# A scan's carry kept in PSUM by writing the capped product one column to the left

## The chip, the cores and the metric

The kernel runs on one core of a Trainium2 chip. The metric is the device time of one launch in microseconds (us); several launches are timed and the median is given. A core has five engines with their own queues: TensorE (PE in the profile) for matrix products, VectorE (DVE), ScalarE (ACT) and GpSimd (POOL) for elementwise work, and SyncE (SP), which here only issues transfers. SBUF is the working memory on the chip, PSUM the small memory into which TensorE writes.

## The reference, cut to what matters

The input has 32 images of 96 channels, 56 x 56 positions. The first layer is a ConvNeXt block: a 7 x 7 convolution per channel, a normalisation over the channels, two dense layers with a GELU between them, and a residual. The second layer, which the change touches, is a 5 x 5 convolution per channel with SiLU, and then a selective scan over the L = 3136 positions of each image, with N = 4 states per channel:

```python
delta = softplus(einsum('dr,brl->bdl', dt_w, dts) + dt_b)
A = -exp(A_logs)
log_dA = maximum(delta[:, :, None, :] * A[None, :, :, None], LOG_EPS)
P = exp(cumsum(log_dA, axis=-1))
dB_u = delta[:, :, None, :] * Bs[:, None, :, :] * xs[:, :, None, :]
hs = P * cumsum(dB_u / maximum(P, EPS), axis=-1)
y = einsum('bdnl,bnl->bdl', hs, Cs) + xs * Ds
```

P is a running product of decays along the positions, and EPS is 1e-9. The kernel carries P/EPS instead of P: where it has fallen below 1, the reference's floor EPS is in force. It computes hs by a recurrence, hs[t] = decay[t] * hs[t-1] + min(P[t]/EPS, 1) * dB_u[t]. The factor with the minimum is called the capped product here.

## The kernel before, in words

The work is done in four stages, one after the other, with intermediate results in HBM: the first convolution, the dense layers (mlp), the second convolution, and the scan. The change is in the scan stage alone.

The scan stage takes each image in two halves of CH = 1568 positions. A step is one half of one image. A pair of images goes together: both first halves, then both second halves. The 96 channels are taken in NG = 3 groups of 32, and 32 channels with 4 states each fill the 128 partitions. One group of one step is a unit: 64 steps x 3 groups make 192 units. Their order has a period of twelve units: six units of first halves (q = 0; two images, three groups), then six of second halves (q = 1).

A unit needs a tile `rep` with two planes: the decay and the drive. It is loaded by SP from HBM (`spread_du`), where delta and delta times x were put before (`keep_du`). ACT turns delta into the decay in three passes (`decay`, L648 to L650). POOL multiplies the drive by B (`drive`, L654). Then DVE does the scan (`scan`): a first scan (L661) forms the running product in the PSUM tile `pv`, with a column of zeros as the other operand; a product with a minimum (L666) caps it, multiplies it by the drive and writes it in place; a second scan (L670) forms hs. In first halves a copy (L665) saves the last column of the running product in `carry_p`, an SBUF tile of six columns, one for each of the six units; the unit of the second half starts its first scan from it. The carry of hs is saved by POOL in `carry_h` (L680).

After that POOL weighs hs with C (`weigh`, L681), PE sums over the states and adds the skip term (`gather`, L687 and L694), and ACT copies the result out of PSUM and issues its store (`store`, L704 and L705). PE also prepares B and C for each step (`rows_bc`, `spread`) and the input of the softplus (`delta_in`); ACT does the softplus (`delta`, L593), POOL the product of delta and x (`delta_x`, L599).

The order is written out by hand. One loop over units, with lead-in and tail, calls these functions at fixed distances: the load four units ahead of the scan, the decay two ahead, the drive one ahead, the weighing one behind. `pin` keeps the order of the calls on each engine. Tiles in pools are reused in turn: five buffers for `rep`, five for hs. The tile `pv` has one buffer of 2048 columns[...]; the running product takes its first 1568 columns and the zero is its last.

Of the kernel before, what the change touches and what calls it, by code (L numbers as in the profile page):

```python
# [8 lines left out]
F32 = mybir.dt.float32  # L9
AF = mybir.ActivationFunctionType  # L10
ALU = mybir.AluOpType
# [21 lines left out]
CH = 1568  # L33
NI = 2
NCH = L // CH
# [3 lines left out]
EPS = 1e-9  # L39
# [3 lines left out]
NG = 3  # L43
# [3 lines left out]
def convnext_then_scan_kernel(  # L47
# [22 lines left out]
    nc = tc.nc  # L70
    pin = tc.keep_in_program_order
# [70 lines left out]
    with tc.tile_pool(name="prep", bufs=1) as prep, tc.tile_pool(  # L142
        name="prep_ps", bufs=1, space=PSUM
# [7 lines left out]
        at = H - 1 - K1 // 2  # L151
# [62 lines left out]
        for k in range(4):  # L214
            rows = slice(32 * k, 32 * k + 2 * N)
            at = 32 * k + (k // 2) * N
# [34 lines left out]
    with tc.tile_pool(name="c1", bufs=3) as pool, tc.tile_pool(  # L251
        name="c1k", bufs=1
# [15 lines left out]
        for c in range(C):  # L268
# [41 lines left out]
            acc2, in0=sq, scalar=-1.0 / C, in1=acc2, op0=ALU.mult, op1=ALU.add  # L310
# [11 lines left out]
    with tc.tile_pool(name="mlp", bufs=2) as pool, tc.tile_pool(  # L322
        name="mlp_h", bufs=3, space=PSUM
# [115 lines left out]
    with tc.tile_pool(name="c2", bufs=3) as pool, tc.tile_pool(  # L439
        name="c2k", bufs=1  # L440
# [93 lines left out]
    with tc.tile_pool(name="sc", bufs=2) as pool, tc.tile_pool(  # L534
        name="sc_k", bufs=1, space=PSUM
    ) as ps_k, tc.tile_pool(name="sc_ps", bufs=2, space=PSUM) as psum:

        pv = ps_k.tile([128, 2048], F32, name="pv")
        nc.vector.memset(pv, 0.0)
        zero = pv[:, 2047:2048].to_broadcast([128, CH])  # L540
        run = pv[:, :CH]
        steps = B * NCH
        units = steps * NG
        xts: dict = {}
# [5 lines left out]
        hss: dict = {}  # L550
        pzs: dict = {}
        pys: dict = {}
        carry_p = pool.tile([128, NI * NG], F32, name="carry_p", bufs=1)
        carry_h = pool.tile([128, NI * NG], F32, name="carry_h", bufs=1)
        HQ = H // NCH

        def place(k):

            p, i = divmod(k, NI)
            return p // NCH * NI + i, p % NCH  # L560
# [95 lines left out]
        def scan(i):  # L656
            k, g = divmod(i, NG)
            q, col = place(k)[1], k % NI * NG + g
            da, ut = (reps[i][:, j, :] for j in range(2))

            pin(nc.vector.tensor_tensor_scan(  # L661
                run, da, zero, carry_p[:, col : col + 1] if q else 1.0 / EPS, ALU.mult, ALU.add
            ))
            if q < NCH - 1:
                pin(nc.vector.tensor_copy(carry_p[:, col : col + 1], run[:, CH - 1 : CH]))  # L665
            pin(nc.vector.scalar_tensor_tensor(  # L666
                run, in0=run, scalar=1.0, in1=ut, op0=ALU.min, op1=ALU.mult
            ))
            ht = pool.tile([128, CH], F32, name=f"hs_{i}", tag="hs", bufs=5)
            pin(nc.vector.tensor_tensor_scan(  # L670
                ht, da, run, carry_h[:, col : col + 1] if q else 0.0, ALU.mult, ALU.add
            ))
            hss[i] = ht
# [41 lines left out]
        for i in range(-12, units + 2):  # L715

            p, at = divmod(i + 8, PER)
# [31 lines left out]
            if 0 <= p < PC and 1 <= at <= 4:  # L749
                j, h = halves[at - 1]  # L750
                delta_x(p * NI + j, h)
            at_unit(i, scan)
            if g == 0 and 0 <= after < steps:
                gather(after, 0)
# [46 lines left out]
```

## Time and profile before

| What | us |
|---|---|
| median of 3 runs | 3668.39 |
| lowest and highest | 3664.61, 3669.38 |
| the profiled execution, its time | 3661.97 |
| the profiled execution, its span | 3660.2 |
| first scan (L661) starts, last scan (L670) ends, in the span | 1888.5, 3646.0 |
| DVE busy in the span | 2670.0 |
| L661, first half / second half, 96 each | 3.428 / 3.489 each |
| L665, 96 | 0.157 each |
| L666, 192 | 1.800 each |
| L670, first half / second half, 96 each | 3.420 / 3.480 each |

The profile is one execution taken by the hardware's profiler. A row names the line of the kernel, the engine, the operation, the tile written, an arrow, and the tiles read; then come shapes and counts, the busy time, and how long the engine stood idle just before and what ended that. An idle time in brackets in a view by time means the same. The span is divided in 40 equal slices in one view, where each digit is the busy share of a slice in tenths.

### The profile page before, as it was taken

How to read it: one execution, taken by the hardware profiler on the slowest of the kernel's cores; microseconds unless marked ns; L12 is line 12 of the kernel's file. 1: busy time of each engine (PE TensorE's matmuls, PEld its weight loads, DVE VectorE, ACT ScalarE, POOL GpSimd, SP SyncE). 2: the span in 40 equal slices, each digit the busy share in tenths (PEclk: the TensorE clock that was granted, in tenths of full speed). 3: DMA queues.
4: the chain of work that ended last, by engine and by line, in shares of the span. 5: the costliest groups of instructions: out<-in, count | busy, mean ns of one | idle time of the engine just before them, and what ended most of it. 6: DMA issues, size and time to landing. Idle time of an engine off the chain costs nothing. (4 is left out here: it accounts for less than half of the span.)

```text
span 3660.2 us, 46554 instructions
## 1 busy us (share of the span) xinstructions
PE 3054.0 (83%) x17290; PEld 1284.6 (35%) x17290; DVE 2670.0 (73%) x1867; ACT 2343.2 (64%) x2133; POOL 1951.4 (53%) x1241
## 2 busy tenths in 40 slices
PE   7999996899999999899948777777777777777775
PEld 5777774333333333334312222222222222222221
DVE  5666665233333333699949999999999999999998
ACT  3555553333333333588858888888888888888884
POOL 2333331122222222100038998898898898898896
PEclk9999998899999999999966666667667667667666
DMA  5555553455555554699977877877877877877873
GB/s 153 167 167 169 168 166 108 150 162 162 160 163 160 162 158 121 183 285 292 289 235 251 276 245 272 275 258 262 272 250 266 277 256 262 278 253 265 278 256 109
DMA packets 302055, 790.70 MB, mean 216 GB/s; under 512 B 123012, under 2 KB 180164, under 8 KB 277156
## 3 DMA queue, kind: packets, MB, share of 16 engines
q1 hardware_dynamic: 259076, 669.31, 56.6%
q0 software_dynamic: 28416, 79.87, 7.2%
q10 hardware_dynamic: 14336, 38.54, 2.8%
q8 instruction: 137, 2.24, 0.3%
q14 instruction: 90, 0.74, 0.1%
HBM read 551.83 MB, written 235.74 MB: 215 GB/s over the span
## 5 line engine op out<-in xcount | busy, mean ns | idle before, releaser
L681 POOL TENSOR_TENSOR hs<-hs,ct 128x1568 f32<-128x1568 f32 x192 | 672.9, 3505 | 102.8 <-DVE hs L670 91.0
L654 POOL TENSOR_TENSOR rep<-rep,bt 128x1568 f32<-128x1568 f32 x192 | 674.5, 3513 | 14.5 <-DMA rep<-du_d 14.5
L382 ACT ACTIVATE g<-ph,b1p_t 128x896 f32<-128x896 f32 x336 | 320.1, 1004 | 512.2 <-PE ph L372 512.2
L402 DVE SCALAR_TENSOR_TENSOR o<-po,b2r_t,x 128x224 f32<-128x224 f32 x336 | 190.5, 609 | 572.3 <-PE po L391 572.3
L286 PE MATMUL ps<-xq,wt 120*112 120x448 f32 x1536 | 581.2, 539 | 14.4 <-POOL xq L281 14.4
L414 POOL DMA_DIRECT2D block_d<-o x336 | 183.0, 552 | 703.8 <-DVE o L402 621.8
L286 PEld LDWEIGHTS ps<-xq,wt 120*112 120x112 f32 x1536 | 429.4, 280 | 165.9 <-POOL xq L281 14.6
L372 PE MATMUL ph<-h,w1r_t 32*128 32x448 f32 x4032 | 440.1, 559 | 55.7 <-DVE h L362 54.0
L599 POOL TENSOR_TENSOR du<-du,xs 96x784 f32<-96x784 f32 x128 | 236.2, 1846 | 367.1 <-ACT du L593 367.1
L585 PE MATMUL pz<-xs,wd_t 96*96 96x392 f32 x512 | 268.6, 688 | 182.6 <-ACT du L593 147.9
L391 PE MATMUL po<-g,w_t 128*32 128x448 f32 x4032 | 413.1, 543 | 0.0
L694 PE MATMUL py<-hs,sel_t 128*32 128x392 f32 x1536 | 330.0, 680 | 85.5 <-POOL hs L681 85.5
L661 DVE TENSOR_TENSOR_SCAN pv<-rep,pv 128x1568 f32<-128x1568 f32 x96 | 329.1, 3428 | 59.9 <-DMA rep<-du_d 43.3
L666 DVE SCALAR_TENSOR_TENSOR pv<-pv,rep 128x1568 f32<-128x1568 f32 x192 | 345.6, 1800 | 21.1 <-POOL hs L681 1.4
L630 PE MATMUL pk<-bn,pick_t 8*128 8x392 f32 x1024 | 284.9, 672 | 87.2 <-ACT y L704 68.1
L661 DVE TENSOR_TENSOR_SCAN pv<-rep,carry_p,pv 128x1568 f32<-128x1568 f32 x96 | 334.9, 3489 | 9.5 <-DVE hs L670 0.5
L670 DVE TENSOR_TENSOR_SCAN hs<-rep,carry_h,pv 128x1568 f32<-128x1568 f32 x96 | 334.1, 3480 | 10.0
L480 PE MATMUL ps<-xq,wt 128*32 128x448 f32 x3072 | 308.4, 547 | 34.2 <-DMA xq<-block_d 31.8
L670 DVE TENSOR_TENSOR_SCAN hs<-rep,pv 128x1568 f32<-128x1568 f32 x96 | 328.4, 3420 | 9.9 <-PE pk L630 0.5
L503 DVE COPY st<-yt 28x896 f32<-28x896 f32 x288 | 317.6, 1103 | 20.6 <-ACT yt L494 8.5
L687 PE MATMUL py<-xs,dsm_t 96*96 96x392 f32 x512 | 318.9, 768 | 14.5 <-ACT bn L618 9.5
L648 ACT ACTIVATE rep<-rep,a_t 128x1568 f32<-128x1568 f32 x192 | 308.4, 1606 | 12.5 <-DMA rep<-du_d 12.2
(87 smaller groups left out, 3473.1 us busy)
## 6 DMA issues: line engine op xcount, KB each, us to landing
rep<-du_d SPq DMA_DIRECT2D x192, 1568.0 KB
du_d<-du SPq DMA_DIRECT2D x128, 588.0 KB
xq<-block_d SPq DMA_DIRECT2D x192, 225.0 KB
block_d<-o POOLq DMA_DIRECT2D x336, 120.0 KB, 5.6
xt<-in_x_dram SPq DMA_DIRECT2D x192, 196.0 KB
h<-conv_d SPq DMA_DIRECT2D x84, 448.0 KB
x<-in_x_dram SPq DMA_DIRECT2D x336, 112.0 KB
conv_d<-st SPq DMA_DIRECT2D x96, 392.0 KB
```

What stands on the lines that cost most here:

```text
L286: nc.tensor.matmul(ps[:, j, :PQ].rearrange("p (i r) -> p i r", i=BI), lhsT=wv[:KR, t], rhs=xq[:KR, j, :, t : t + W2], start=(t == 0), stop ...
L372: pin(nc.tensor.matmul(phs[i // 2][:, i % 2, :HALF], lhsT=w1r_t[rows, d, f * 128 : (f + 1) * 128], rhs=hts[n, d][rows, s * HALF : (s + 1) ...
L382: nc.scalar.activation(gt, ph[:, :, :HALF], AF.Gelu, bias=b1p_t[:, f : f + 1], scale=1.0)
L391: pin(nc.tensor.matmul(po[CB * i : CB * i + CB, :HALF], lhsT=w2_t[:, f, CB * d : CB * d + CB], rhs=gts[n, s, f, i // 2][:, i % 2], start=( ...
L503: pin(copy(st[:, :, :, :, f], yt[RW * f : RW * f + QR].rearrange("p h (b q) -> p h b q", q=QW),))
L654: pin(nc.gpsimd.tensor_mul(ut, ut, bts[i // NG]))
L661: pin(nc.vector.tensor_tensor_scan(run, da, zero, carry_p[:, col : col + 1] if q else 1.0 / EPS, ALU.mult, ALU.add))
L666: pin(nc.vector.scalar_tensor_tensor(run, in0=run, scalar=1.0, in1=ut, op0=ALU.min, op1=ALU.mult))
L670: pin(nc.vector.tensor_tensor_scan(ht, da, run, carry_h[:, col : col + 1] if q else 0.0, ALU.mult, ALU.add))
L681: pin(nc.gpsimd.tensor_mul(ht, ht, cts[k]))
L687: pin(nc.tensor.matmul(half(py[:C], s), lhsT=dsm_t, rhs=tokens(k, 2 * h + s, 4), start=True, stop=False,))
L694: pin(nc.tensor.matmul(py[g * DG : (g + 1) * DG, s, :BK], lhsT=sel_t, rhs=hss[k * NG + g][:, cols], start=False, stop=True, tile_position= ...
```

## The change

The running product is written one column to the right of where the capped product is put. Let `at` be the column at which the capped product begins. The first scan writes columns `at + 1` to `at + 1568`, and the product with the minimum reads these and writes `at` to `at + 1567`. So the last column of the running product, `at + 1568`, is left as it was. In first halves `at` is 6, 5, 4, 3, 2 and 1 for the six units in their order, so each unit's last column lies just behind the columns that the later units use, and the six carries stand in columns 1569 to 1574. In second halves `at` is 0, and the highest column written is 1568. The first scan of a second half takes its start value from the unit's column in PSUM. The tile `carry_p` and the copy into it are gone. The zero stays in column 2047. After the change the first scan has line 664, the product line 667, the second scan line 671.

```diff
-        run = pv[:, :CH]
...
-        carry_p = pool.tile([128, NI * NG], F32, name="carry_p", bufs=1)
...
             da, ut = (reps[i][:, j, :] for j in range(2))
+            at = 0 if q else NI * NG - col
+            run, grown = pv[:, at : at + CH], pv[:, at + 1 : at + 1 + CH]
+            last = NI * NG - col + CH
 
             pin(nc.vector.tensor_tensor_scan(
-                run, da, zero, carry_p[:, col : col + 1] if q else 1.0 / EPS, ALU.mult, ALU.add
+                grown, da, zero, pv[:, last : last + 1] if q else 1.0 / EPS, ALU.mult, ALU.add
             ))
-            if q < NCH - 1:
-                pin(nc.vector.tensor_copy(carry_p[:, col : col + 1], run[:, CH - 1 : CH]))
             pin(nc.vector.scalar_tensor_tensor(
-                run, in0=run, scalar=1.0, in1=ut, op0=ALU.min, op1=ALU.mult
+                run, in0=grown, scalar=1.0, in1=ut, op0=ALU.min, op1=ALU.mult
             ))
```

## The prediction

> **What bounds the kernel now.** I read the strip of 40 slices first, to find the stage that the change touches, and then asked for the busy time of each engine between the first scan's start and the last scan's end.
>
> ```profile
> DVE  5666665233333333699949999999999999999998
> ```
> ```profile
> 1888.50:3646.00 1757.50, 1308.11 (x4536) 409.94 (x4536) 1687.07 (x672) 1427.04 (x1202) 1574.53 (x602) 0.67 0.77 259
> ```
>
> The columns of the second fence are the window, its length, then busy time and count of PE, weight loads, VectorE (DVE), ScalarE (ACT) and GpSimd (POOL), the clock, the DMA share and GB/s. In the scan stage DVE is busy 1687.1 of 1757.5 us (96%), POOL 90%, ACT 81%, PE 74%, DMA 77%. The rest of DVE's time is mostly the step from one instruction to the next, so I went to its order of time.
>
> ```profile
> 2597.66 3.43 DVE L661 TENSOR_TENSOR_SCAN pv<-rep,pv 128x1568 f32<-128x1568 f32 x1
> 2601.12 0.16 DVE L665 COPY carry_p<-pv 128x1 f32<-128x1 f32 x1
> 2601.39 1.80 DVE L666 SCALAR_TENSOR_TENSOR pv<-pv,rep 128x1568 f32<-128x1568 f32 x1
> 2603.29 3.42 DVE L670 TENSOR_TENSOR_SCAN hs<-rep,pv 128x1568 f32<-128x1568 f32 x1
> 2606.80 3.49 DVE L661 TENSOR_TENSOR_SCAN pv<-rep,carry_p,pv 128x1568 f32<-128x1568 f32 x1
> 2610.39 1.80 DVE L666 SCALAR_TENSOR_TENSOR pv<-pv,rep 128x1568 f32<-128x1568 f32 x1
> 2612.30 3.48 DVE L670 TENSOR_TENSOR_SCAN hs<-rep,carry_h,pv 128x1568 f32<-128x1568 f32 x1
> ```
>
> Columns: start, duration, engine, line. The first four lines are a unit of an image's first half, with the copy; the last three one of a second half, with no copy but with two carries read. Nothing in brackets stands behind them: no idle time that another engine ended. Units follow one another every 9.137 us (first half) and 9.067 us (second half), medians over the starts. Each run of twelve units (a cycle: two images, three groups, two halves) has six of each. Waits on others are few: DVE stood still 43.3 us ahead of the first scan, 7.46 us ahead of the second, and then some eight times for about 0.45 us. So a nanosecond taken from DVE's chain is a nanosecond of the span, until another engine is late.
>
> [...] 103 to 104 ns pass between any of the large instructions. [...] No scan of the kernel before reads its carry from PSUM. [...] a copy of one column out of PSUM takes 157 ns, and a copy of five columns from SBUF 159 ns.
>
> **The change part by part.**
>
> *Removed: 96 copies (L665).* The page's row gives 157 ns each, 15.1 us in all. But the slot is longer than the row. From the end of the scan to the start of the product (L666) it is 34 + 157 + 104 ns, 296 ns with rounding, in units with the copy, and 104 ns in units without (medians over 96 each). So the change takes 296 - 104 = 192 ns, and 96 x 0.192 = 18.4 us.
>
> *Changed: 96 scans read the carry from PSUM.* A carry from SBUF costs 3489 - 3428 = 61 ns in this scan, and 3480 - 3420 = 60 ns in the other. From below, the PSUM pointer could be free: -61 ns, -5.9 us. [...] I take 0, because where the trace has both kinds of source they cost alike: the copies above[...].
>
> *Moved: the product is written one column left of what it reads, 192 times; in first halves the tile also starts one to six columns later.* Lengths and steps are unchanged. [...] Below, nothing is to be gained from an address. Above, the rate could halve (rival 3). I take 0.
>
> *Waits and queues.* In the built program PE, ACT, POOL and SP have the same instructions in the same order with the same kinds of waits. DVE has 96 fewer, and each remaining scan and product waits for what it waited for. The first scan still waits for the DMA that brought its operands, for DVE's own last scan and for ACT; the product for POOL; the second scan for PE. No DMA is added or moved. The copy had no reader outside DVE.
>
> *What is late next.* The saving comes in six units in a row, 6 x 0.192 = 1.15 us a cycle, and POOL and ACT have to follow. In the first half, POOL has this to do in a unit that also makes the product of delta and x:
>
> ```profile
> 2670.32 0.18 POOL L680 COPY carry_h<-hs 128x1 f32<-128x1 f32 x1 [0.24 <-DVE hs L670]
> 2670.58 3.49 POOL L681 TENSOR_TENSOR hs<-hs,ct 128x1568 f32<-128x1568 f32 x1
> 2674.04 3.52 POOL L654 TENSOR_TENSOR rep<-rep,bt 128x1568 f32<-128x1568 f32 x1
> 2677.49 1.86 POOL L599 TENSOR_TENSOR du<-du,xs 96x784 f32<-96x784 f32 x1
> 2679.46 0.18 POOL L680 COPY carry_h<-hs 128x1 f32<-128x1 f32 x1
> ```
>
> That is 9.03 us to the end of L599, 9.14 to the next start. DVE's unit becomes 9.137 - 0.192 = 8.945 us, so over three such units POOL falls some 0.1 to 0.15 us a unit behind. It makes that up in the units without L599, where it waits 1.9 us. What DVE needs of POOL (L654, for the product) was ready 5.0 us or more ahead in every unit, so this costs nothing directly. But it delays the weighing (L681), the gather on PE and, behind that in ACT's queue, the exponentials. The tightest of these is the one for a cycle's eighth unit, which ACT makes after the softplus of the next images and two table loads:
>
> ```profile
> 2722.17 1.60 ACT L650 ACTIVATE rep<-rep,lift_t 128x1568 f32<-128x1568 f32 x1
> ```
> ```profile
> 2725.10 3.49 DVE L661 TENSOR_TENSOR_SCAN pv<-rep,carry_p,pv 128x1568 f32<-128x1568 f32 x1
> ```
>
> It ends at 2723.78, 1.32 us before the scan that reads it. Over the sixteen cycles this margin is 0.03 us in the first, 0.35 and 0.36 in the next two, then 1.3 to 2.4 in twelve. DVE will come 1.15 us sooner, ACT's chain perhaps 0.2 us (its start, the third unit's weighing, gains 3 x 0.192 less POOL's lag of about 0.4). So the first cycle loses all of its 1.15 us, the next two 0.6 us each, and the others keep about 0.3 us in hand. Lost: 2.3 us.
>
> *Sum.* 18.4 - 2.3 = 16.1 us. Against the profiled execution, which ran 3661.97 us (span 3660.2, 1.8 us around it): 3645.9 us. The median of the three runs, 3668.39, is 6.4 us above that execution, and I predict the median: 3668.4 - 16.1 = 3652 us.
>
> **The rivals.**
>
> *1. POOL sets the pace in the first half.* If it holds its four units with L599 at the old 9.13 us and DVE has to wait there, only two of six copies count: 96 x 2/6 x 0.192 = 6.1 us, 3662 us. For it: POOL is nearly without a pause in these units. Against it: the 5 us of lead that L654 has, and POOL's 1.9 us of waiting in the units after. The same result follows if ACT's margin is lost in most cycles.
>
> *2. The carry from PSUM costs[...].* [...] At 192 ns more per scan it would eat all of the saving[...].
>
> *3. Slower: reading and writing PSUM one column apart collide.* [...] It decides from 16.1 us / 192 = 84 ns per product on, that is from 1.88 us. For it: the mlp stage's result operation (L402), the same kind with a PSUM source at a step of two columns, takes 609 ns for 224 columns[...]. Against it: here the step stays one[...].
>
> That the change doesn't do what it says is excluded for the count of instructions; whether the copy's slot closes is what the units without it show.
>
> **How the numbers follow.** Bounds first: this kernel's three runs lie within 0.13%, and a change under 0.2% (7.3 us) can't be told from none. The forecast, with the pointer anywhere in its bounds (rival 2 is its upper part), has 0.85: from 3668.4 - 16.1 - 5.9 = 3646[...]. Rival 1 has 0.06 and gives 3662, which is no difference. Rival 3 or a smaller cost of the same kind has 0.09. Faster 0.85, same 0.06, slower 0.09. The range 3641 to 3662 leaves out rival 3, part of rival 1 and a little below.
>
> **What the profile after would show.** No row for carry_p. The product 104 ns behind every scan, at 1800 ns; first-half units every 8.945 us and second-half units every 9.067. The scan with a carry at 3489 ns[...]. The stretch from the first scan to the last at 1741 us instead of 1757.4. DVE's waits for ACT's L650 up from 7.9 to about 10 us; POOL's idle ahead of L680 and L681 (73.6 + 91.0 us) down by about the saving. The prediction is wrong if the product's or a scan's row grows, or if waits for POOL or ACT appear in most cycles.

## The result, and the profile after

The changed kernel is faster: 3651.77 us median (3650.18 to 3655.9, 6 runs) against 3665.89 us (3664.52 to 3669.38, 6 runs, those shown before among them). The ratio is 0.9960, with a 95% interval of 0.9950 to 0.9971. That is 14.1 us less, about twice the 0.2% below which I had counted a change as none.

The profiled execution ran 3655.9 us, the slowest of the six. Its first scan starts at 1896.5 us instead of 1888.5. The stages ahead of it are the same program in both kernels, and in the second profile of the changed kernel below it starts at 1893.6 us, so I don't count this difference as the change's. I compare the stretch from the first scan's start to the last scan's end instead. Here is that stretch in the changed kernel (window, length, busy time and count of PE, weight loads, DVE, ACT and POOL, clock, DMA share, GB/s):

```profile
1896.50:3639.10 1742.60, 1309.79 (x4536) 410.16 (x4536) 1672.42 (x576) 1426.93 (x1202) 1572.60 (x602) 0.67 0.78 261
```

The stretch is 1742.6 us instead of 1757.5, 14.9 us less. DVE lost 96 instructions and 14.7 us of busy time (1687.1 to 1672.4). By time, a unit of a first half and one of a second half now look like this (start, duration, engine, line):

```profile
2599.30 3.43 DVE L664 TENSOR_TENSOR_SCAN pv<-rep,pv 128x1568 f32<-128x1568 f32 x1
2602.83 1.80 DVE L667 SCALAR_TENSOR_TENSOR pv<-pv,rep 128x1568 f32<-128x1568 f32 x1
2604.74 3.42 DVE L671 TENSOR_TENSOR_SCAN hs<-rep,pv 128x1568 f32<-128x1568 f32 x1
2608.25 3.49 DVE L664 TENSOR_TENSOR_SCAN pv<-rep,pv 128x1568 f32<-128x1568 f32 x1
2611.85 1.80 DVE L667 SCALAR_TENSOR_TENSOR pv<-pv,rep 128x1568 f32<-128x1568 f32 x1
2613.76 3.48 DVE L671 TENSOR_TENSOR_SCAN hs<-rep,carry_h,pv 128x1568 f32<-128x1568 f32 x1
```

The product follows the scan directly, and its duration is the old one although it now reads one column and writes the one before it. In this and the other comparisons below I use medians over the 96 units of a kind, and "waits" for the time by which the units exceed those medians:

| Scan stage, us | before | after | after, second profile |
|---|---|---|---|
| first scan's end to product, first half | 0.296 | 0.104 | 0.104 |
| first-half unit, start to start | 9.137 | 8.947 | 8.946 |
| first scan with a carry | 3.489 | 3.493 | 3.493 |
| second-half unit, start to start | 9.067 | 9.071 | 9.072 |
| waits over the stage, from the first scan on | 9.95 | 12.94 | 12.73 |
| stretch, first scan to last | 1757.4 | 1742.6 | 1742.4 |

The account closes. The copies' slots give 96 x 0.190 = 18.2 us, the carry from PSUM takes back 95 x 0.004 = 0.4 us, and the waits take back 3.0 us: 14.8 us. What DVE waits for is named in the view of waits (us in total, times, longest), cut to DVE's lines:

```profile
DVE pv L664 <- ACT rep L650: 54.2, 5, 43.8
DVE pv L667 <- POOL hs L682: 1.4, 3, 0.5
DVE hs L671 <- DVE pv L667: 1.4, 3, 0.5
DVE pv L664 <- DVE hs L671: 0.9, 2, 0.4
DVE pv L664 <- DMA rep<-du_d: 0.4, 1, 0.4
```

The 43.8 us are the start of the stage, put down to a DMA in the kernel before. What remains on ACT is 10.4 us, against 7.9 before: 7.92 us ahead of the second unit, and three waits of 0.6 to 1.0 us.

Unit by unit, the 3.0 us have three parts. About 1.9 us are at the eighth unit of a cycle: 2.2 us in three cycles, against 0.34 us in one before. About 0.5 us are ahead of the second unit, and 0.7 us are two more of some short pauses that come at even distances (see the end). In the second profile the parts are about 0.65, 1.5 and 0.7 us. So the sum repeats, and its parts do not. The wait ahead of the second unit differs in this way without the change too: by the same measure it is 7.31 us before, and 8.64 and 8.63 us in the first two experiments, where ACT has the same work and the copy is still made. A difference of a microsecond between two stretches can be that alone.

### The profile page after: what moved, and what is told of

It is laid out like the page before. It is cut to its first block, busy times and chain, and to the rows that moved or that the text cites. A ratio compares the mean times of both kernels' runs of the same rounds, so it can differ in the third digit from the quotient of the medians.

```text
span 3654.1 us, 46458 instructions
## 1 busy us (share of the span) xinstructions
PE 3060.6 (84%) x17290; PEld 1286.4 (35%) x17290; DVE 2655.5 (73%) x1771; ACT 2341.0 (64%) x2133; POOL 1950.5 (53%) x1241
## 5 line engine op out<-in xcount | busy, mean ns | idle before, releaser
L664 DVE TENSOR_TENSOR_SCAN pv<-rep,pv 128x1568 f32<-128x1568 f32 x192 | 664.5, 3461 | 72.2 <-ACT rep L650 54.2
L402 DVE SCALAR_TENSOR_TENSOR o<-po,b2r_t,x 128x224 f32<-128x224 f32 x336 | 190.4, 608 | 572.4 <-PE po L391 572.4
L286 PE MATMUL ps<-xq,wt 120*112 120x448 f32 x1536 | 581.9, 540 | 14.1 <-POOL xq L281 14.1
L585 PE MATMUL pz<-xs,wd_t 96*96 96x392 f32 x512 | 277.3, 707 | 172.0 <-ACT du L593 139.1
L671 DVE TENSOR_TENSOR_SCAN hs<-rep,carry_h,pv 128x1568 f32<-128x1568 f32 x96 | 334.0, 3479 | 10.4 <-DVE pv L667 0.5
L688 PE MATMUL py<-xs,dsm_t 96*96 96x392 f32 x512 | 308.6, 746 | 11.7 <-ACT bn L618 6.1
L649 ACT ACTIVATE rep<-rep,lift_t 128x1568 f32<-128x1568 f32 x192 | 307.6, 1602 | 6.2
```

Source lines behind the costliest of these rows:

```text
L286: nc.tensor.matmul(ps[:, j, :PQ].rearrange("p (i r) -> p i r", i=BI), lhsT=wv[:KR, t], rhs=xq[:KR, j, :, t : t + W2], start=(t == 0), stop ...
L664: pin(nc.vector.tensor_tensor_scan(grown, da, zero, pv[:, last : last + 1] if q else 1.0 / EPS, ALU.mult, ALU.add))
L671: pin(nc.vector.tensor_tensor_scan(ht, da, run, carry_h[:, col : col + 1] if q else 0.0, ALU.mult, ALU.add))
```

## The experiments

All ratios are to the kernel before, run on the same chip.

**The layout alone.** The shifted layout, with the copy and its SBUF tile put back. The edit is to the changed kernel.

```diff
+        carry_p = pool.tile([128, NI * NG], F32, name="carry_p", bufs=1)
...
-                grown, da, zero, pv[:, last : last + 1] if q else 1.0 / EPS, ALU.mult, ALU.add
+                grown, da, zero, carry_p[:, col : col + 1] if q else 1.0 / EPS, ALU.mult, ALU.add
...
+            if q < NCH - 1:
+                pin(nc.vector.tensor_copy(carry_p[:, col : col + 1], grown[:, CH - 1 : CH]))
```

> The changed layout alone: the product is written one column left of the running product, but the copy into carry_p stays and the carry is read from SBUF. My theory (the whole gain is the copy's slot on DVE): no gain and no loss against before, ratio 0.999 to 1.001; the product at 1.800 us in all 192 units, 296 ns from the first scan's end to the product's start, first-half units every 9.137 us. Rival (the shift is itself faster or dearer): rows of the product or of a scan that differ from 1.800, 3.428, 3.489 or 3.420/3.480 us by more than 5 ns.

Measured: ratio 1.0000 (0.9991 to 1.0009). The product takes 1.800 us, the scans 3.428, 3.489, 3.420 and 3.480, the slot 296 ns and the unit 9.137 us. Here, writing one column to the left of what is read cost nothing and gained nothing.

**The carry's place alone.** The old layout, with the copy going to PSUM.

```diff
-        carry_p = pool.tile([128, NI * NG], F32, name="carry_p", bufs=1)
+        carry_p = pv[:, 1600 : 1600 + NI * NG]
```

> The old layout with the copy, but the copy goes to a column of PSUM behind the running product and the second half's scan reads its carry from there. My theory: the pointer in PSUM costs 4 ns more than in SBUF (the scan 3.493 us instead of 3.489), 96 x 0.004 = 0.4 us, ratio 1.000; the copy's row near 157 ns. [...]

Measured: ratio 1.0006 (0.9997 to 1.0015). The scan with a carry takes 3.493 us, as in the changed kernel, against 3.489 in the kernel before, so the pointer in PSUM costs 4 ns more than in SBUF. The copy's row, which now writes to PSUM, is 167 ns instead of 157, and first-half units come every 9.146 us.

**The copy twice.** The kernel before, with the line of the copy repeated.

```diff
                 pin(nc.vector.tensor_copy(carry_p[:, col : col + 1], run[:, CH - 1 : CH]))
+                pin(nc.vector.tensor_copy(carry_p[:, col : col + 1], run[:, CH - 1 : CH]))
```

> The kernel before with the copy made twice in a row, the second behind the first by its wait. My theory (a copy on the bounding engine costs its slot, row plus 34 ns, and nothing hides it): 96 x 0.19 = 18.3 us more than before, ratio 1.0050, first-half units every 9.328 us, and the waits for ACT at the eighth unit of a cycle no more than before. Rival A (only the row of 157 ns counts): 15.1 us, 9.294 us a unit. Rival B (the copy hid behind waits on other engines, and the change gained for another reason): under 5 us.

Measured: 3683.68 us, ratio 1.0049 (1.0034 to 1.0064). By time:

```profile
2600.00 3.43 DVE L661 TENSOR_TENSOR_SCAN pv<-rep,pv 128x1568 f32<-128x1568 f32 x1
2603.47 0.16 DVE L665 COPY carry_p<-pv 128x1 f32<-128x1 f32 x1
2603.66 0.16 DVE L666 COPY carry_p<-pv 128x1 f32<-128x1 f32 x1
2603.92 1.80 DVE L667 SCALAR_TENSOR_TENSOR pv<-pv,rep 128x1568 f32<-128x1568 f32 x1
```

The second copy starts 0.19 us behind the first, and the product 488 ns behind the scan's end instead of 296. First-half units come every 9.330 us, and the stretch is 18.5 us longer. So one more copy costs its slot of 0.19 us and nothing hides it; the row of 157 ns alone would have given 9.294 us. That copies hid behind waits on other engines, rival B of the expectation, falls.

**ACT relieved.** Both kernels without ACT's third pass over the decay, to see whether what was lost went to ACT. The edit is the same in both. The decay is then 1e-9 smaller than it should be.

```diff
             pin(nc.scalar.activation(da, da, AF.Relu, bias=lift_t[:, 0:1], scale=1.0))
-            pin(nc.scalar.activation(da, da, AF.Identity, bias=lift_t[:, 1:2], scale=1.0))
```

> The kernel before without ACT's third pass over the decay (L650, which adds EPS back), so ACT has 192 x 1.6 us less to do in the scan stage; the decay is left 1e-9 too small. My theory: DVE is the bound with ACT nowhere near it, so the stretch from the first scan to the last loses only the waits on ACT, some 8 us of 1757.4, about 1749 us; no waits of DVE on ACT after the first two units.

> The changed kernel without ACT's third pass over the decay, as in the run beside it. My theory (the 3 us by which the gain fell short of 18.2 are DVE's waits on ACT, at the eighth unit of some cycles and at the start): no waits of DVE on ACT after the first two units, and the stretch from the first scan to the last shorter than in the kernel before with the same pass left out by the full 96 x (0.190 - 0.004) = 17.9 us, about 1731 us. Rival (POOL holds DVE back in the first half): the difference stays at 15 us and first-half units come out above 8.947 us.

Measured: the kernel before this way is at ratio 0.9995 (0.9986 to 1.0003), the changed kernel at 0.9951 (0.9934 to 0.9969). The stretches are 1755.85 and 1738.63 us. My figure for the kernel before was wrong: I had counted all of its 8 us of waits as ACT's to give back, but the wait ahead of the second unit stays (about 6 us), and the small ones of 0.45 us are not ACT's (see the end). It gained 1.6 us only. The comparison that mattered came out near: the two stretches differ by 17.2 us, where 17.9 was expected by my theory and 15 by the rival, and first-half units come every 8.946 us, not more. DVE is put down as waiting for ACT once after the first two units, for 0.44 us, at one of the even distances described at the end. The waits of the two differ by 0.83 us instead of 3.0: two more of the pauses, and 0.17 us ahead of the second unit. At the eighth unit nothing is left; ACT is done there at least 1.43 us ahead in every cycle. So some 2.2 of the 3.0 us come back when ACT is relieved.

**The changed kernel again.** No edit; a second profile.

> The changed kernel once more, for a second profile. My theory: the stretch from the first scan to the last within 1 us of the 1742.6 us of its first profile, with the waits on ACT in a few cycles, not the same ones; the start of the first scan may lie some us earlier or later, since the stages ahead of it are the same program as before.

Measured: 3651.87 us, the stretch 1742.4 us. The margin between ACT's last pass and the scan of the eighth unit, cycle by cycle, is 1.94, 1.50, 0.58, 0.03, 2.38, 1.81, 1.33, 3.43 us and so on in the first profile, and 1.84, 1.40, 0.03, 2.78, 1.99, 1.43, 3.91, 0.51 in this one. It runs out (0.03) in the fourth, twelfth and thirteenth cycle there, and in the third and fifteenth here.

**The weighing in a tile of its own.** The edit is to the changed kernel. There the second scan waits for PE, because PE reads the tile of hs that it will overwrite. If POOL writes the weighed values elsewhere, PE's reading no longer concerns the scan, and what POOL has read is known from the product's wait for POOL.

```diff
-            ht = pool.tile([128, CH], F32, name=f"hs_{i}", tag="hs", bufs=5)
+            ht = pool.tile([128, CH], F32, name=f"hs_{i}", tag="hs", bufs=2)
...
-            pin(nc.gpsimd.tensor_mul(ht, ht, cts[k]))
+            wt = pool.tile([128, CH], F32, name=f"hw_{i}", tag="hw", bufs=4)
+            pin(nc.gpsimd.tensor_mul(wt, ht, cts[k]))
+            hss[i] = wt
```

> The changed kernel, but POOL's weighing writes a tile of its own (four buffers) instead of hs in place (two buffers now), so the second scan no longer has to wait for PE and is left with one wait, on DVE itself. My theory (the step of 104 ns between large DVE instructions is 34 ns plus 70 ns for a second wait, as the first five units, whose second scan has no wait on PE, show): 34 ns ahead of the second scan everywhere, 187 x 0.07 = 13.1 us less than the changed kernel, so some 3639 us and 0.9925 of before, less what waits on ACT and POOL take back. Rival ([...]whatever the waits): still 104 ns, the time of the changed kernel, 0.996 of before.

Measured: 3632.43 us, ratio 0.9909 (0.9894 to 0.9924), the fastest of all kernels here. The view of the line of the second scan in the changed kernel has, besides the scans, a row of the queue's own waiting instructions (count, then shortest, median and longest duration in ns, first and last start in us):

```profile
L671 DVEq EVENT_SEMAPHORE  x187: 21/21/21, 1954.1 to 3635.5; - x187
```

In this kernel that view has no such row, and by time the second scan follows at once:

```profile
2606.37 1.80 DVE L667 SCALAR_TENSOR_TENSOR pv<-pv,rep 128x1568 f32<-128x1568 f32 x1
2608.21 3.48 DVE L671 TENSOR_TENSOR_SCAN hs<-rep,carry_h,pv 128x1568 f32<-128x1568 f32 x1
2611.78 3.49 DVE L664 TENSOR_TENSOR_SCAN pv<-rep,pv 128x1568 f32<-128x1568 f32 x1
```

The step is 34 to 36 ns instead of 103 to 104, and units come every 8.875 and 9.003 us. That is 96 x 0.072 + 95 x 0.068 = 13.4 us of the 18.0 us by which the stretch shrinks (1742.6 to 1724.6). The other 4.5 us are waits: they fell from 12.9 to 8.4 us. Some 2.2 us of that are the waits at the eighth unit, where the margin is now at least 0.97 us in every cycle; about as much is that three of the pauses show instead of nine, and the rest is ahead of the second unit. POOL's weighing starts 0.20 us behind the scan in first halves, instead of 0.33 to 0.43, because it no longer waits for the copy of the carry of hs: its row starts before that of the copy has ended. Whether this is why ACT's margin holds is open. In the next run the weighing starts as early, and the margin comes down to 0.08 us in the fourteenth cycle.

**The same edit on the kernel before.** To see whether it works without the change, and what the copy is worth then.

> The kernel before, with the copy, and with the weighing in a tile of its own as in the run e6. My theory (the second wait of the second scan costs 70 ns a unit whatever else is done, and the copy 0.19 us a unit of a first half): 34 ns ahead of the second scan, units every 9.067 and 8.997 us, a stretch of about 1743.5 us from the first scan to the last, 0.996 of before; and against e6 (1724.6 us) more by the copies' full 96 x (0.190 - 0.004) = 17.9 us plus at most 1 us of waits. Rival (in e6 the gain of 18 us came from a shorter chain through POOL and PE, which the kernel before did not need): a gain well under 13 us here.

Measured: 3653.16 us, ratio 0.9967 (0.9955 to 0.9978). The step is 34 to 35 ns, units come every 9.071 and 8.999 us, the stretch is 1743.26 us, 14.2 us less than before. So the second wait of the second scan costs its 70 ns in either kernel. Against the run above, the copies are worth 18.65 us of the stretch. The waits are nearly the same in the two (8.6 and 8.4 us), and first-half units are 0.196 us apart, 18.8 us in all, less 0.4 us for the pointer: where nothing else is late, the whole of the slots is gained.

## Why the prediction was right, point by point

**The bound.** DVE is the bound of the stage: a copy more costs 18.5 us, a copy less gains 14.9 or, where nothing else is late, 18.65.

**The copy's slot.** Predicted 192 ns and 18.4 us, measured 190 ns a unit and 18.2 us. Reading the slot off the units without a copy, rather than the row of 157 ns, was the step that mattered. That POOL would hold the first half at its old pace, rival 1, is out: those units come every 8.947 us instead of 9.137, and what the product needs of POOL was still ready 5.06 us or more ahead.

**The carry in PSUM.** I took 0, with -61 ns as the bound from below; measured +4 ns, 0.4 us: the changed kernel and the copy into PSUM alone both show 3.493 us, where the carry in SBUF gave 3.489. The bound from above, on which rival 2 and the upper end of the range rested, was an assumption that no trace shows. The 192 ns more per scan that would have eaten all of the saving are far off.

**The shift.** I took 0, and the layout alone shows 0 (ratio 1.0000). Rival 3 is out: the product stayed at 1.800 us, and it would have taken 1.88 or more. That the step of two columns is what makes L402 slow, 609 ns for 224 columns, was my assumption; no run shows it.

**What is late next.** The term was 2.3 us, all of it at the eighth unit. The waits grew by 3.0 us, and of these 1.9 us are at the eighth unit in the first profile and 0.65 in the second; the wait ahead of the second unit and the pauses were not in the working. The place was right: the three ACT waits beyond the stage's start are at the eighth unit, as here, where the last pass starts at 2291.00 us, takes 1.60, and the scan follows it:

```profile
2291.00 1.60 ACT L650 ACTIVATE rep<-rep,lift_t 128x1568 f32<-128x1568 f32 x1
```
```profile
2292.63 3.49 DVE L664 TENSOR_TENSOR_SCAN pv<-rep,pv 128x1568 f32<-128x1568 f32 x1 [0.96 <-ACT rep L650]
```

But the working behind the number was wrong in its detail. I carried the margin of each cycle over from the kernel before, so that the first three cycles would lose. In the changed kernel the first three kept 1.94, 1.50 and 0.58 us; the fourth, twelfth and thirteenth ran out. The margin is no property of the cycle: with the layout alone, where no time was saved, it is smallest in the ninth (0.19 us). That the size of the term came near is therefore luck. POOL's lag was mis-sized too: 0.1 to 0.15 us a unit was predicted; the weighing starts 0.329, 0.367 and 0.428 us behind the scan in the first three units, 0.04 to 0.06 a unit. POOL's named waits for the second scan fell by 9.5 us (73.6 + 91.0 to 62.1 + 93.0), less than "about the saving".

**The step between instructions.** I read 103 to 104 ns between any two large instructions, as one price that all of them pay. That was wrong twice, though the sum does not rest on it. Ahead of a first scan the step is 89 to 91 ns; the lines that I showed have it too (2603.29 + 3.42 to 2606.80). And the last two experiments show that 70 of the 104 ns ahead of a second scan are a second wait. What a first wait costs no run decides, since every DVE instruction of the scan stage has at least one. Nor does the kernel before have such a step everywhere. In its mlp stage 81 products (L362) follow a result operation (L402), 79 of them with a wait for another engine only, and each starts 75 to 96 ns before the row ahead of it ends.

**The sum.** 16.1 us was predicted and 14.1 us measured. The base, 3668.39 us, was the median of three runs; over six it is 3665.89. The two misses, some 2 us each, cancel, so that 3652 against 3651.77 is closer than the working deserves: that much is luck.

## What to carry to other kernels

DVE bounds the stage here, and a copy on it cost the 190 ns by which it delayed the next instruction, not the 157 ns of its row. So look for the same sequence with and without it in one trace and subtract. Then look at the waits that each instruction carries: here the second scan paid 70 ns in each of 187 units for a second one. Choosing which engine frees a buffer was worth 18.0 us of the stretch in the changed kernel and 14.2 in the kernel before, as much as the 14.9 from removing the copies.

## What I had not expected

A second wait on the second scan costs 70 ns: the step ahead of it is 34 to 36 ns with one wait and 103 to 104 with two. In the kernel before and in the changed one, the second scans of the first five units have no wait for PE, and they show the 34 ns without any edit. With the second wait the second scan has an instruction of its own for waiting in DVE's queue, 187 in all in the changed kernel: it starts 38 to 39 ns after the instruction before has ended, and its row is 21 ns. The product has two waits and 104 ns as well, but no run takes its second wait away. It is not so that each wait adds 70 ns. The first scan has three, for a DMA, for DVE and for ACT, and a step of 89 to 91 ns only. Its waiting instruction stands in the queue while the second scan still runs, as its length in the changed kernel tells:

```profile
L664 DVEq EVENT_SEMAPHORE  x195: 49/3451/3493, 1891.6 to 3626.5; - x195
```

Whether the 70 ns are for the second wait as such, or for a wait that is for another engine, these runs do not separate. Taking it off the second scan shortened the stretch by 18.0 us in the changed kernel, side effects included, and by 14.2 us in the kernel before, about as much as the change studied here.

DVE stands still for about 0.45 us at even distances, whichever engine the profile names. In the changed kernel such waits start the instructions at 2039.27, 2232.54, 2424.74, 2617.68 us and so on, every 193 us; before the change they came every 180 us or a multiple of that, and with the weighing apart every 229 or a multiple: some do not show. A unit has 6.5, 6 and 5 instructions in DVE's queue in these three kernels (waiting instructions counted), so each time it is 128 of them. Counted in the traces, the distances are exactly 128 instructions in the changed kernel and multiples of 128 in the other two. I had read these as waits on other engines. What happens there, no run shows.
